# A two-layer graph network on one core: other step orders in both layers, and the last group's row sums as columns

## The chip, the core and the metric

One core of a Trainium2 chip runs the whole program. The metric is the device time of one execution in microseconds; of several runs of a kernel the median is given. One more execution was taken by the hardware profiler; all rows below are from that one.

## The reference

The inputs are x (128 graphs of 128 nodes with 512 features, float32) and adj (128 matrices of 128x128). Two layers follow each other:

```
# layer 0
agg = (adj @ x) / max(rowsum(adj), 1e-6)
x   = layernorm(x + relu(concat(x, agg) @ W.T))
# layer 1
e   = leaky_relu(sj[None, :] + si[:, None] + ab, 0.2)     # scores of x @ Wv + bv with aw
T   = adj * exp(e);  T = T / (rowsum(T) + 1e-12)
H   = x @ Wk[0] + bk[0] + (T @ x) @ Wk[1] + bk[1] + (T @ T @ x) @ Wk[2] + bk[2]
out = layernorm(x + relu(H))
```

Everything is float32.

## The kernel before, in words

**Tiling.** The 128 graphs are taken in 32 groups of four (`G`, `NG`). Group n of 0 to 31 is layer 0, of 32 to 63 layer 1. The 512-feature products use a seven-product (Strassen-like) scheme on two levels: the outer one has the products P12, P56, P74 and `last` (the steps "t") in layer 0, and O1, O2, O5, O6, O7, O4, O3 in layer 1; each of these has seven inner products, its steps 1 to 7. One step is a matmul (or two) and the instruction of VectorE (DVE), ScalarE (ACT) or both that takes its result out of PSUM. One float32 matmul shows in the trace as two passes.

**Banks.** PSUM's eight banks are two lanes of four, `lanes[0]` (bB) and `lanes[1]` (bA). A product calls its lane's banks X, Y, W, Z. In `outer` (line 617) step 1 writes X, and ACT copies X to Y (L628); step 2 writes Z, copied to s5 (L634); step 3 adds to X, and DVE makes W = X + s5 (L637); step 4 finishes Y, which is evicted; step 5 adds to X again, and DVE takes X out (L663 or L676); step 6 finishes W, step 7 X. So step 3 must wait for step 1's copy, step 5 for step 3's add, step 7 for step 5's read. O5 begins with a copy of the bias into X (L626). In `last` (layer 0) X and Z are the two halves of one bank, Y and W of another: t.1 writes X (read by L397), t.2 Z (L400, L401), t.3 X (L404), t.5 X (L409), t.7 X (L416); t.8 to t.11 multiply with the graph's matrix, and `residual` (L380) takes them out.

**Layer 1's second half, `combine` (the steps "c").** For each graph b: `one(b)` multiplies with T into a bank, DVE adds two pieces of the product's result to it and writes v1 (L829, L830), and ACT copies a third piece into the bank (L831); `two(b)` multiplies v1 with T on top of that piece. Group g's steps c run inside group g + 1's list, those of the last group at the end of its own, where they are called x.1 to x.8 (PL).

**The order of the work.** Nothing is left to a scheduler: every engine executes its instructions in program order, and that order is written out. The lists PF, PA (layer 0), PT (last layer-0 group and start of layer 1), PG, PB (layer 1) and PL (last group) give the order of the steps. All other work (transposes `x_turn`, sums `x_inner`, `x_s1` to `x_s4`, degrees, normalisations, loads and stores) is hung between the steps by the PLACES tables: a number is a slot counted from the start of the group's list, two slots to a step; the even slot lies right behind the step's own instructions, the odd one behind the instructions that the step defers (`late`). PA has 32 steps (64 slots), PB 57 (114); a slot beyond that falls into a later group. DMAs are all issued on SyncE (SP) in that same order. PLACES_S (around the change of layers), PLACES_L (last group), PLACES_M and PLACES_T (loads of the second layer's weights) replace or add places.

**The last group's end.** There is no time for a round trip through memory for the scores, so `end_scores` (from L746) makes the diagonal of si (L730), spreads it over all partitions by a matmul with ones, and ACT makes exp of the scores with sources on partitions (L752, L754). `end_rows` multiplies with the adjacency (L760) and spreads the row sums over all partitions, again by a matmul with ones, 256 columns for each half (two graphs). `end_norm` adds epsilon (L768), takes the reciprocal of all 128x256 numbers (L769) and multiplies (L770). Then come x.1 to x.8, the statistics and the stores.

**Start.** Line 151 multiplies the identity into all eight banks once.

Of the kernel before, what the change touches and what calls it, by code (L numbers as in the profile page):

```python
# [16 lines left out]
def kernel(  # L17
# [15 lines left out]
    P = 128  # L33
# [25 lines left out]
    def need(*keys):  # L59
        for k in keys:  # L60
            assert k in done, k
# [89 lines left out]
    for t in bA + bB:  # L151
        nc.tensor.matmul(t, ident, ident[:, None, :].to_broadcast([P, Q, P]), start=True, stop=True)
# [603 lines left out]
    def end_rows(g, h):  # L756
        need(("end_scores", g), ("adj_turn",))
        T = TTs[g][:, 2 * h : 2 * h + 2].rearrange("p b n -> p (b n)")
        pt = lanes[0][1 + h][:, :FH]
        V.tensor_mul(T, T, adjs[2 * NG - 1][:, 2 * h : 2 * h + 2].rearrange("p b n -> p (b n)"))  # L760
        mm(pt, ones[:].to_broadcast([P, P]), T, True)

    def end_norm(g, h):
        need(("end_rows", g, h))
        T = TTs[g][:, 2 * h : 2 * h + 2].rearrange("p b n -> p (b n)")
        pt = lanes[0][1 + h][:, :FH]
        rr = halves()[:, :FH]
        V.tensor_scalar(rr, pt, ROW_EPS, None, ALU.add)  # L768
        V.reciprocal(rr, rr)  # L769
        V.tensor_mul(T, T, rr)  # L770
# [41 lines left out]
    def combine(lane, g):  # L812
        n = NG + g
        X, Y, W, Z = lane
        at_ = {0: X, 1: Z, 2: W, 3: Y}
# [8 lines left out]
        def one(b):  # L824
            need(("end_norm", g, b // 2) if g == NG - 1 else ("t_turn", g))
            need(("O4" if b > 1 else "O3", g, 7), ("sum_c", g, 0), ("sum_c", g, 1))
            mm(at_[b], TTs[g][:, b], row(b, 0, F, 0), True)
            v = v1[b] = v1s[(g * G + b) % 3]
            V.tensor_add(v[:, :258], at_[b][:, :258], row(b, F, 2 * BW, 0))  # L829
            V.tensor_add(v[:, 258:], at_[b][:, 258:], row(b, 0, 254, 1))  # L830
            L_.copy(at_[b], row(b, 254, 766, 1))  # L831

        def two(b):
            mm(at_[b], TTs[g][:, b], v1[b])
            late.append((residual, n, b, at_[b]))
# [15 lines left out]
    def step(lane, name, g, k):  # L851
# [3 lines left out]
    PA = "p74.5 P12.1 P12.2 p74.6 P12.3 p74.7 P12.4 t.1 P12.5 P12.6 t.2 P12.7 P56.1 t.3 P56.2 t.4 t.5 P56.3 t.6 t.7 t.8 t.9 t.10 t.11 P74.1 P74.2 P56.4 P56.5 P56.6 P74.3 P56.7 P74.4".split()  # L855
    PT = "p74.5 p74.6 O1.1 O1.2 O1.3 p74.7 O1.4 t.1 O1.5 O1.6 t.2 O1.7 O2.1 t.3 O2.2 t.4 t.5 O2.3 t.6 t.7 t.8 t.9 t.10 t.11 O2.4 O2.5 O2.6".split()
    PG = ("O5.1 O5.2 O5.3 O5.4 O2.5 O2.6 O6.1 O6.2 O5.5 O5.6 O5.7 O7.1 O6.3 O6.4 O7.2 "
          "O6.5 O2.7 O7.3 O6.6 O7.4 O6.7 O4.1 O4.2 O7.5 O4.3 O7.6 O7.7 O4.4 c.1 O4.5 "
          "O4.6 c.2 c.3 c.4 O4.7 O3.1 O3.2 O3.3 O3.4 c.5 c.6 c.7 c.8 O3.5 O3.6").split()
    PB = ("O1.1 o3.7 O1.2 O1.3 O2.1 O1.4 O1.5 O1.6 O2.2 O1.7 O2.3 O2.4 O5.1 O5.2 O2.5 O5.3 O2.6 O5.4 O2.7 "  # L860
          "O6.1 O5.5 O6.2 O5.6 O6.3 O5.7 O6.4 O7.1 O6.5 O6.6 O7.2 O7.3 O6.7 O4.1 O7.4 O7.5 O4.2 O4.3 O7.6 "
          "O4.4 O4.5 O7.7 c.1 O4.6 O4.7 O3.1 O3.2 c.2 O3.3 c.3 c.4 c.5 c.6 c.7 c.8 O3.4 O3.5 O3.6").split()
    PL = ("O1.1 o3.7 O1.2 O2.1 O1.3 O2.2 O1.4 O1.5 O1.6 O1.7 O2.3 O2.4 O5.1 O2.5 O5.2 O2.6 O2.7 O5.3 O5.4 O6.1 O5.5 O6.2 "
# [44 lines left out]
    def place_op(n, pos, name, m, *a):  # L908
# [3 lines left out]
        else:  # L912
# [3 lines left out]
        ("ln_apply", -2, 3): 4, ("ln_var", -2, 0): -9, ("sum_c22", -2): -40, ("ln_scales", -2): -1, ("ln_mean", -2): -15,  # L916
        ("ln_var", -2, 2): -4, ("load_y", -2, 1): -27, ("ln_apply", -2, 2): 10, ("ln_var", -2, 1): -4,
        ("load_y", -2, 0): -31, ("x_s4", -1): -36, ("ln_var", -2, 3): -12, ("x_s1", -1): -66, ("a_load", -2): -65,
        ("a_turn", -2): -36, ("x_s3", -1): -52, ("y_store", -2, 1): 25, ("ln_apply", -2, 1): 15, ("x_turn", 0, 0, 1): -20,
        ("y_store", -2, 0): 32, ("ln_apply", -2, 0): 15, ("load_left", 0, 0): -49, ("ln_apply", -1, 3): 68, ("x_s2", 0): 28,  # L920
        ("x_turn", 0, 1, 1): -37, ("load_adj", 0): 154, ("ln_var", -1, 0): 58, ("sum_c22", -1): 21, ("ln_scales", -1): 62,
        ("ln_mean", -1): 48, ("x_turn", 0, 0, 0): -28, ("ln_var", -1, 2): 55, ("load_y", -1, 1): 38, ("load_y", -1, 0): 40,
        ("ln_var", -1, 1): 55, ("ln_apply", -1, 2): 70, ("x_s1", 0): 5, ("x_turn", 0, 1, 0): -39, ("a_load", -1): 7,
        ("x_turn", 1, 0, 1): 55, ("x_inner", 0, 0): -12, ("a_norm", -1): -23, ("ln_var", -1, 3): 58, ("degree", -1): -48,
        ("a_turn", -1): 27, ("x_s3", 0): 19, ("y_store", -1, 1): 95, ("ln_apply", -1, 1): 79, ("x_inner", 0, 1): -29,
        ("y_store", -1, 0): 100, ("ln_apply", -1, 0): 82, ("load_left", 1, 0): 9, ("x_s1", 1): 97, ("x_turn", 1, 0, 0): 41,
        ("x_s2", 1): 99, ("x_s4", 0): 80, ("load_left", 1, 1): -24, ("x_inner", 1, 1): 61, ("x_turn", 1, 1, 0): 32,
        ("x_s3", 1): 127, ("x_inner", 1, 0): 64, ("x_turn", 1, 1, 1): 47, ("x_s2", -1): -44,
    }
    PLACES_A = {  # L930
        ("x_s4", 0): 35, ("ln_apply", 0, 3): 131, ("x_s2", 1): 86, ("x_turn", 1, 1, 1): 33, ("ln_var", 0, 0): 124,
        ("sum_c22", 0): 87, ("ln_scales", 0): 126, ("w_slot", 0, 1): 24, ("ln_mean", 0): 113, ("x_turn", 1, 0, 0): 33,
        ("ln_var", 0, 2): 124, ("load_y", 0, 1): 100, ("ln_var", 0, 1): 118, ("load_y", 0, 0): 100, ("ln_apply", 0, 2): 134,
        ("x_s1", 1): 67, ("x_turn", 1, 1, 0): 28, ("a_load", 0): 73, ("x_inner", 1, 0): 51, ("a_norm", 0): 36,
        ("ln_var", 0, 3): 115, ("degree", 0): 17, ("load_left", 2, 1): 38, ("w_slot", 0, 0): 4, ("a_turn", 0): 90,
        ("x_s3", 1): 83, ("y_store", 0, 1): 157, ("ln_apply", 0, 1): 140, ("x_turn", 1, 0, 1): 42, ("x_inner", 1, 1): 36,
        ("load_adj", 1): 37, ("y_store", 0, 0): 161, ("ln_apply", 0, 0): 138, ("load_left", 2, 0): 78,
    }
    PLACES_B = {
        ("t_norm", 0): 154, ("sum_r", 0, 1): 81, ("load_y", 0, 0): 170, ("ln_var", 0, 3): 230, ("x_turn", 1, 0, 1): 19,  # L940
        ("t_back", 0): 165, ("x_s1", 1): 66, ("ln_scales", 0): 239, ("t_sums", 0): 149, ("x_turn", 1, 1, 1): 19,
        ("load_left", 2, 0): 82, ("ln_var", 0, 1): 227, ("y_store", 0, 0): 264, ("t_turn", 0): 187, ("ln_var", 0, 2): 224,
        ("sum_c", 0, 0): 109, ("ln_apply", 0, 2): 273, ("ln_apply", 0, 3): 257, ("x_inner", 1, 1): 53, ("ln_var", 0, 0): 235,
        ("t_exp", 0): 140, ("load_left", 2, 1): 70, ("ln_apply", 0, 1): 257, ("y_store", 0, 1): 278, ("x_s2", 1): 68,
        ("x_turn", 1, 1, 0): -5, ("x_s3", 1): 97, ("ln_apply", 0, 0): 242, ("t_load", 0): 123, ("t_scores", 0): 119,
        ("x_turn", 1, 0, 0): 14, ("sum_r", 0, 0): 86, ("x_s4", 0): 42, ("load_adj", 0): 103, ("load_y", 0, 1): 190,
        ("ln_mean", 0): 223, ("sum_c", 0, 1): 115, ("x_inner", 1, 0): 41,
    }
    PLACES_M = {
        ("ln_mean",): 212, ("ln_apply", 3): 234, ("ln_var", 1): 219, ("ln_apply", 0): 250, ("y_store", 0): 251,  # L950
        ("ln_apply", 2): 231, ("ln_var", 2): 225, ("ln_apply", 1): 235, ("ln_var", 3): 225, ("ln_scales",): 230,
        ("y_store", 1): 244, ("ln_var", 0): 227,
    }
    PLACES_L = {
        ("end_store", 2): 158, ("sum_c", 1): 72, ("sum_r", 0): 71, ("end_store", 0): 158, ("t_scores",): 105,
        ("end_var", 1): 134, ("sum_r", 1): 71, ("load_adj",): 96, ("load_y", 0): 47, ("end_apply", 1): 160,
        ("load_y", 1): 106, ("end_mean", 1): 128, ("end_rows", 0): 111, ("end_mean", 0): 127, ("end_rstd", 2): 132,
        ("end_store", 1): 160, ("end_apply", 2): 137, ("end_stats", 2): 129, ("end_store", 3): 162, ("end_scales",): 140,
        ("sum_c", 0): 76, ("end_rstd", 3): 149, ("end_apply", 0): 144, ("end_scores",): 106, ("end_rows", 1): 111,
        ("end_norm", 0): 111, ("end_stats", 3): 138, ("end_norm", 1): 111, ("end_apply", 3): 158, ("adj_turn",): 96,  # L960
        ("end_var", 0): 131,
    }
    OPS = {f.__name__: f for f in (load_left, load_y, load_adj, x_turn, x_inner, x_s1, x_s2, x_s3, x_s4, sum_c22, degree, a_norm, a_load, a_turn, w_slot, ln_mean, ln_var, ln_scales, ln_apply, y_store, sum_r, sum_c, t_scores, t_load,
           t_exp, t_sums, t_norm, t_back, t_turn, end_scores, end_rows, end_norm)}
    ENDS = {f.__name__: f for f in (adj_turn, end_mean, end_var, end_scales, end_stats, end_rstd, end_apply, end_store)}
    LAST = {"ln_mean", "ln_var", "ln_scales", "ln_apply", "y_store"}
    OWN = {"sum_r", "sum_c", "t_scores", "t_load", "t_exp", "t_sums", "t_norm", "t_back", "t_turn", "end_scores", "end_rows", "end_norm"}
# [112 lines left out]
```

## Time and profile before

| what | value |
|---|---|
| median of 3 runs | 2085.56 us (2084.93 to 2086.3) |
| profiled execution: time | 2083.08 us |
| profiled execution: span from first to last instruction | 2081.3 us |
| mean granted TensorE clock | 0.998 |
| PE, DVE, POOL, ACT busy | 99%, 73%, 66%, 56% |
| one group of layer 0, from 137.37 us | 24.74 us |
| one group of layer 1, from 887.61 us | 38.91 us |
| DMA | 287.13 MB, mean 138 GB/s |

A timeline row gives the start (us), the time it covers, engine, line, operation, what is written and read (buffer numbers left out), the shape and the count; a bracket at its end is the idle time of that engine before it and the instruction that ended it. PE is the matmul, PEld the load of its weights. A row of the waits is: engine and line that waited, the one that it waited for, us in total, number of times, longest.

### The profile page before, as it was taken

What the parts mean: (1) busy time and instruction counts of PE and PEld (TensorE: products, weight loads), DVE (VectorE), ACT (ScalarE), POOL (GpSimd) and SP (SyncE); (2) the same over time, 40 slices, a digit from 0 to 9 for tenths busy, and PEclk for the clock granted to TensorE, in tenths of its full rate; (3) what the DMA queues carried; (4) which work ended last, traced back from release to release, by engine and by line L of the source; (5) the groups of instructions that cost most, each with busy time, mean ns of one, the idle gap of its engine ahead of it and who ended that gap; (6) DMA issues with size and microseconds to landing.
All of it is one profiled execution on the core that took longest, in us unless ns stands there. A gap on an engine that the chain in (4) does not pass through costs nothing.

```text
span 2081.3 us, 25875 instructions
## 1 busy us (share of the span) xinstructions
PE 2062.5 (99%) x7096; PEld 1329.9 (64%) x7096; DVE 1525.8 (73%) x3414; ACT 1155.7 (56%) x2875; POOL 1377.7 (66%) x1263
## 2 busy tenths in 40 slices
PE   9999999999999999999999999999999999999997
PEld 6778888888878886555555555555555555555553
DVE  6777777777777777676776776776776776776766
ACT  2656666666666666355455455455455465465464
POOL 5877888887676776656656656656556556556552
PEclk9999999999999999999999999999999999999999
DMA  9776666666667776435434535535535435435423
GB/s 206 174 190 194 180 182 179 160 187 192 163 160 190 190 183 218 107 87 122 116 87 115 124 87 127 112 87 128 111 87 130 109 87 132 107 87 132 107 67 117
DMA packets 431070, 287.13 MB, mean 138 GB/s; under 512 B 155593, under 2 KB 353865, under 8 KB 430924
## 3 DMA queue, kind: packets, MB, share of 16 engines
q1 hardware_dynamic: 429996, 284.15, 54.6%
q10 hardware_dynamic: 800, 1.31, 0.3%
q8 instruction: 56, 0.92, 0.2%
q14 instruction: 90, 0.74, 0.1%
q0 software_dynamic: 128, 0.01, 0.0%
HBM read 191.60 MB, written 93.79 MB: 137 GB/s over the span
## 4 chain that ended last, share of the span: by engine, by line
PE 97%; DVE 1%; DMA 1%; ACT 0%; issue 0%; POOL 0%; SPq 0%; ACTq 0%; DVEq 0%
PE bA L155 51%; PE bB L155 46%; DMA yd<-y 0%; DMA xb<-in_x_dram 0%; DMA y<-in_x_dram 0%; PE bA L181 0%; DVE s L769 0%; DVE y L380 0%; POOL r L709 0%; ACT y L517 0%; DVE big L995 0%; DVE xl L259 0%; DVE xu L259 0%; DVE big L1003 0%; SPq L83 0%
## 5 line engine op out<-in xcount | busy, mean ns | idle before, releaser
L155 PE MATMUL bB<-big,xu 128*128 128x385 f32 (+1 forms) x1806 | 569.5, 435 | 1.0 <-DVE c L676 0.7
L155 PEld LDWEIGHTS bB<-big,xu 128*128 128x128 f32 x1806 | 339.4, 190 | 166.6 <-issue 30.1
L155 PE MATMUL bA<-big,xl 128*128 128x256 f32 (+1 forms) x1358 | 395.9, 416 | 0.3 <-DVE bA L475 0.3
L155 PE MATMUL bB<-big,xs 128*128 128x256 f32 (+1 forms) x1316 | 388.8, 416 | 0.0
L155 PEld LDWEIGHTS bA<-big,xl 128*128 128x128 f32 x1358 | 256.8, 189 | 100.1 <-issue 15.5
L155 PEld LDWEIGHTS bB<-big,xs 128*128 128x128 f32 x1316 | 249.5, 190 | 84.2 <-issue 1.7
L155 PE MATMUL bA<-big,xu 128*128 128x256 f32 (+1 forms) x896 | 290.0, 435 | 0.2
L155 PE MATMUL bA<-c,TT 128*128 128x512 f32 x512 | 245.9, 592 | 3.0 <-DVE c L669 1.9
L504 ACT ACTIVATE junk<-y,mv 128x512 bf16<-128x512 f32 x252 | 181.3, 719 | 72.7 <-POOL mv L499 68.5
L155 PEld LDWEIGHTS bA<-big,xu 128*128 128x128 f32 x896 | 165.4, 189 | 82.2 <-DVE bA L637 9.7
L517 ACT ACTIVATE y<-y,mv,rstd 128x512 f32<-128x512 f32 x252 | 201.5, 812 | 1.4 <-POOL mv L512 1.4
L380 DVE SCALAR_TENSOR_TENSOR y<-bA,y 128x512 f32<-128x512 f32 x256 | 170.4, 683 | 19.6 <-PE bA L155 13.4
L155 PE MATMUL bA<-big,xs 128*128 128x385 f32 x448 | 178.3, 492 | 0.0
L709 POOL TENSOR_TENSOR r<-r,s 128x770 f32<-128x770 f32 x64 | 115.1, 1820 | 86.4 <-DVE c L669 86.4
L155 PE MATMUL bB<-big,xl 128*128 128x385 f32 (+1 forms) x462 | 167.2, 480 | 0.5 <-ACT bA L456 0.4
L155 PEld LDWEIGHTS bA<-c,TT 128*128 128x128 f32 x512 | 96.8, 189 | 93.0 <-issue 48.1
L790 POOL TENSOR_TENSOR T<-ag,T 128x512 f32<-128x512 f32 x31 | 39.5, 1275 | 175.9 <-ACT T L785 175.9
L499 POOL TENSOR_SCALAR mv<-mv 128x4 f32<-128x4 f32 x63 | 14.5, 230 | 212.3 <-DVE y L380 212.3
L270 POOL TENSOR_TENSOR xs<-xl 128x896 f32<-128x896 f32 x63 | 131.4, 2086 | 23.9 <-PE bB L155 23.9
L282 POOL TENSOR_TENSOR xu<-xu,xs 128x896 f32<-128x896 f32 x63 | 131.8, 2091 | 8.8 <-PE bB L155 8.8
L831 ACT COPY bA<-r 128x512 f32<-128x512 f32 x64 | 37.7, 590 | 176.4 <-DVE big L830 170.7
L637 DVE TENSOR_TENSOR bB<-bB,s 128x385 f32<-128x385 f32 x128 | 72.5, 567 | 85.1 <-PE bB L155 75.4
(190 smaller groups left out, 3636.7 us busy)
## 6 DMA issues: line engine op xcount, KB each, us to landing
xb<-in_x_dram SPq DMA_DIRECT2D x256, 128.0 KB, 3.8
y<-in_x_dram SPq DMA_DIRECT2D x64, 512.0 KB, 4.3
yd<-y SPq DMA_DIRECT2D x64, 512.0 KB, 3.0
xb<-yd SPq DMA_DIRECT2D x256, 128.0 KB, 5.8
y<-yd SPq DMA_DIRECT2D x64, 512.0 KB, 5.9
out_dram<-y SPq DMA_DIRECT2D x62, 512.0 KB, 2.8
ag<-in_adj_dram SPq DMA_DIRECT2D x63, 256.0 KB, 5.9
sb<-sd SPq DMA_DIRECT2D x252, 64.0 KB, 3.2
```

Of the source, the lines that this page charges most:

```text
L155: nc.tensor.matmul(dst, lhsT, rhs, start=start, stop=True, skip_group_check=True)
L270: S_.tensor_add(xs[n][:, 0], xl[n][:, 0], xl[n][:, 1])
L282: S_.tensor_sub(xu[n][:, 1], xu[n][:, 1], xs[n][:, 1])
L380: V.scalar_tensor_tensor(y, t, 0.0, y, ALU.max, ALU.add, accum_out=mvs[n][:, b, 0:1])
L499: S_.tensor_scalar(mvs[n][:, :, 0], mvs[n][:, :, 0], -1.0 / F, None, ALU.mult)
L504: L_.activation(junk, ys[n, b // 2][:, b % 2], AF.Square, bias=mvs[n][:, b, 0:1], accum_out=mvs[n][:, b, 1:2])
L517: L_.activation(y, y, AF.Identity, bias=mvs[n][:, b, 0:1], scale=rstds[n][:, b : b + 1])
L637: V.tensor_add(W, X, s5)
L709: S_.tensor_add(r, r, s)
L790: S_.tensor_mul(T, adjs[NG + g], T)
L831: L_.copy(at_[b], row(b, 254, 766, 1))
```

## The change

- PF and START are as they were. PA, PT, PG, PB and PL contain the same steps in another order, and the numbers of the PLACES tables are set anew.
- The last group's row sums: `end_rows` now multiplies with the one-column `ones` as moving operand, so the sums of one graph are one column on the partitions of the rows, four columns in one bank. `end_recip` (new) adds epsilon and takes reciprocals of 128x2 numbers and writes two diagonals; `end_norm` spreads those by a matmul with ones (256 columns, same bank) and multiplies from PSUM.
- `end_base` (new): for graphs 0, 1 and 2 of the last group the third piece is put into banks of the other lane by a matmul with the identity ahead of time; `two(b)` adds to it there. The ACT copy L831 remains for graph 3 in that group and everywhere in the others.
- The matmul of the identity at the start covers seven banks, not eight.

```diff
-    for t in bA + bB:
+    for t in bA + bB[:3]:
...
     def end_rows(g, h):
-        need(("end_scores", g), ("adj_turn",))
+        need(("end_scores", g), ("adj_turn",), *[("end_rows", g, 0)] * h)
+        T, pt = TTs[g], lanes[0][0]
+        t2 = T[:, 2 * h : 2 * h + 2].rearrange("p b n -> p (b n)")
+        V.tensor_mul(t2, t2, adjs[2 * NG - 1][:, 2 * h : 2 * h + 2].rearrange("p b n -> p (b n)"))
+        for b in (2 * h, 2 * h + 1):
+            mm(pt[:, b : b + 1], T[:, b], ones, b == 0)
+
+    def end_recip(g, h):
+        need(("end_rows", g, 1))
+        t = lanes[0][0][:, 2 * h : 2 * h + 2]
+        rr = small.tile([P, 2], FP, name="rr2")
+        V.tensor_scalar(rr, t, ROW_EPS, None, ALU.add)
+        V.reciprocal(rr, rr)
+        if h == 0:
+            ends["dr"] = p1.tile([P, G, N], FP, name="dr", tag="sb")
+        for b in (0, 1):
+            V.tensor_scalar(ends["dr"][:, 2 * h + b], ident, rr[:, b : b + 1], None, ALU.mult)
+
+    def end_norm(g, h):
+        need(("end_recip", g, 1), *[("end_norm", g, 0)] * h)
         T = TTs[g][:, 2 * h : 2 * h + 2].rearrange("p b n -> p (b n)")
...
+        pt = lanes[0][0][:, h * FH : (h + 1) * FH]
+        mm(pt, ones[:].to_broadcast([P, P]), ends["dr"][:, 2 * h : 2 * h + 2].rearrange("p b n -> p (b n)"), h == 0)
+        V.tensor_mul(T, T, pt)
+
+    def end_base(g, b):
+        need(("sum_c" if b > 1 else "O3", g, 0 if b > 1 else 7))
+        t = (rs[NG + g], last22[g])[b // 2][:, b % 2].rearrange("p n m -> p (n m)")
+        mm(lanes[0][1 + b], ident, t[:, 254:766], True)
...
-        at_ = {0: X, 1: Z, 2: W, 3: Y}
+        at_ = to = {0: X, 1: Z, 2: W, 3: Y}
+        if g == NG - 1:
+            to = {0: lanes[0][1], 1: lanes[0][2], 2: lanes[0][3], 3: X}
...
-            L_.copy(at_[b], row(b, 254, 766, 1))
+            if g < NG - 1 or b == 3:
+                L_.copy(to[b], row(b, 254, 766, 1))
 
         def two(b):
-            mm(at_[b], TTs[g][:, b], v1[b])
-            late.append((residual, n, b, at_[b]))
+            need(*[("end_base", g, b)] if g == NG - 1 and b < 3 else [])
+            mm(to[b], TTs[g][:, b], v1[b])
+            late.append((residual, n, b, to[b]))
...
-    PA = "p74.5 P12.1 P12.2 p74.6 P12.3 p74.7 P12.4 t.1 P12.5 P12.6 t.2 P12.7 P56.1 t.3 P56.2 t.4 t.5 P56.3 t.6 t.7 t.8 t.9 t.10 t.11 P74.1 P74.2 P56.4 P56.5 P56.6 P74.3 P56.7 P74.4".split()
+    PA = "p74.5 P12.1 p74.6 P12.2 P12.3 p74.7 t.1 P12.4 P12.5 t.2 P12.6 P12.7 P56.1 t.3 P56.2 t.4 t.5 P56.3 t.6 t.7 t.8 t.9 t.10 t.11 P74.1 P56.4 P74.2 P56.5 P56.6 P74.3 P56.7 P74.4".split()
-    PT = "p74.5 p74.6 O1.1 O1.2 O1.3 p74.7 O1.4 t.1 O1.5 O1.6 t.2 O1.7 O2.1 t.3 O2.2 t.4 t.5 O2.3 t.6 t.7 t.8 t.9 t.10 t.11 O2.4 O2.5 O2.6".split()
+    PT = "p74.5 p74.6 O1.1 O1.2 O1.3 p74.7 t.1 O1.4 O1.5 O1.6 t.2 O1.7 O2.1 t.3 O2.2 t.4 t.5 t.6 O2.3 t.7 t.8 O2.4 O2.5 t.9 O2.6 t.10 t.11".split()
...
-    PB = ("O1.1 o3.7 O1.2 O1.3 O2.1 O1.4 O1.5 O1.6 O2.2 O1.7 O2.3 O2.4 O5.1 O5.2 O2.5 O5.3 O2.6 O5.4 O2.7 "
-          "O6.1 O5.5 O6.2 O5.6 O6.3 O5.7 O6.4 O7.1 O6.5 O6.6 O7.2 O7.3 O6.7 O4.1 O7.4 O7.5 O4.2 O4.3 O7.6 "
-          "O4.4 O4.5 O7.7 c.1 O4.6 O4.7 O3.1 O3.2 c.2 O3.3 c.3 c.4 c.5 c.6 c.7 c.8 O3.4 O3.5 O3.6").split()
+    PB = ("O1.1 o3.7 O1.2 O1.3 O2.1 O1.4 O1.5 O2.2 O1.6 O1.7 O2.3 O2.4 O5.1 O5.2 O2.5 O5.3 O2.6 O5.4 O5.5 "
+          "O2.7 O6.1 O5.6 O6.2 O6.3 O5.7 O6.4 O7.1 O6.5 O6.6 O7.2 O6.7 O7.3 O4.1 O7.4 O7.5 O4.2 O4.3 O7.6 "
+          "O4.4 O4.5 O7.7 O4.6 c.1 O4.7 O3.1 c.2 c.3 O3.2 c.4 c.5 c.6 O3.3 c.7 c.8 O3.4 O3.5 O3.6").split()
```

Of the places, those that the prediction speaks of (slot before, slot after). PLACES_A: degree 17, 19; x_turn (1,1,0) 28, 26; x_turn (1,1,1) 33, 30; x_turn (1,0,0) 33, 32; a_turn 90, 95 (26, 31 of the next group); a_load 73, 81; load_left (2,0) 78, 93; sum_c22 87, 80. PLACES_B: x_turn (1,0,1) 19, 29; x_turn (1,1,0) -5, -5; t_scores 119, 121; t_load 123, 126; t_sums 149, 151; t_norm 154, 154; t_back 165, 167; t_turn 187, 189; y_store (0,1) 278, 284; load_left (2,0) 82, 88. PLACES_L: end_scores 106, 108; end_base (2), (0), (1) new at 110, 111, 112; end_rows 111, 111; end_recip new at 111, 112; end_norm (0) 111, 113, (1) 111, 115. In PG, O4.5 to O4.7 read `O4.5 O4.6 ... O4.7` before (the steps c between them are empty in that group) and `O4.5 O7.7 O4.6 ... O4.7` after.

## Prediction

> **What bounds the kernel now.** I read the page first, then the waits of PE's weight loads, then the timeline of one steady group of each layer and of the end.
>
> ```profile
> span 2081.3 us, 25875 instructions
> PE 2062.5 (99%) x7096; PEld 1329.9 (64%) x7096; DVE 1525.8 (73%) x3414; ACT 1155.7 (56%) x2875; POOL 1377.7 (66%) x1263
> ```
>
> TensorE is the bound. A pass over 256, 385 or 512 columns takes 216, 324 or 430 ns from start to start (eight of 256 from 143.84 to 145.57; six of 385 from 890.96 to 892.90; two of 512 from 920.22 to 921.07), and a float32 product is two passes. Counting all passes at that price gives 2038 us, so 43 us of the span is not passes: 9 lie behind the last product, some 19 in waits at the start, at the change of layers and in the last group, and 15 in tiny waits that come back in each group of a layer (0.16 x 31 and 0.33 x 30, below). Most of those never show as idle PE. They show on the weight load: when a semaphore comes so late that the weights are not loaded ahead, a pass is some 100 ns late.
>
> ```profile
> PEld bA L155 <- ACT bA L831: 23.8, 37, 1.6
> PEld bB L155 <- DVE r L676: 14.1, 30, 0.8
> ...
> PEld bA L155 <- DVE s L401: 8.8, 31, 0.3
> ```
>
> The middle number is the count: 30 or 31 is once a group. Layer 0, one group:
>
> ```profile
> 146.38 0.16 DVE L599 TENSOR_REDUCE deg<-deg 128x4 f32<-128x8 f32 x1 [0.62 <-ACT junk L597]
> 146.86 1.03 PE L155 MATMUL bB<-big,xs 128*128 128x256 f32 x4
> 147.32 0.41 DVE L401 TENSOR_TENSOR s<-bA,s 128x256 f32<-128x256 f32 x1
> 147.78 0.30 PEld L155 LDWEIGHTS bA<-big,xu 128*128 128x128 f32 x2 [0.29 <-DVE s L401]
> 147.78 0.70 PE L155 MATMUL bA<-big,xu 128*128 128x256 f32 x2
> 148.32 1.03 PE L155 MATMUL bB<-big,xs 128*128 128x256 f32 x4
> ```
>
> Step P56.1 starts at 146.86 and needs 4 x 0.216, so t.3 could start at 147.72; it starts at 147.78, and its two passes last 0.54, not 0.43. Sum 0.16 us a group. The cause is the first row: `degree` stands in DVE's order ahead of t.2's two adds (L400, L401), and DVE sits 0.62 us waiting for ACT's sums.
>
> Layer 1, one group:
>
> ```profile
> 887.06 0.70 DVE L259 STREAM_TRANSPOSE xl<-xb 128x512 f32<-128x512 f32 x1
> 887.69 0.52 DVE L676 TENSOR_TENSOR r<-bB,r 128x385 f32<-128x385 f32 x1
> 888.26 0.30 PEld L155 LDWEIGHTS bB<-big,xu 128*128 128x128 f32 x2 [0.46 <-DVE r L676]
> ...
> 894.92 0.50 ACT L626 COPY bA<-beta 128x385 f32<-128x385 f32 x1
> 895.57 1.53 PE L155 MATMUL bA<-big,xs 128*128 128x385 f32 x4
> ...
> 897.79 0.56 DVE L676 TENSOR_TENSOR c<-bB,c 128x385 f32<-128x385 f32 x1
> 898.43 0.57 DVE L637 TENSOR_TENSOR bA<-bA,s 128x385 f32<-128x385 f32 x1
> ```
>
> Three places: o3.7 waits for L676 behind a transpose (0.10 us), O5.1 for the bias copy L626 behind the copy out of O1.7 (0.16), c.8 for c.5's copy L831 (six passes from 883.03 to 885.67 take 2.64 against 2.58: 0.07). The end:
>
> ```profile
> 2060.43 1.75 DVE L769 RECIPROCAL s<-s 128x256 f32<-128x256 f32 x1
> 2062.70 1.13 PE L155 MATMUL bA<-c,TT 128*128 128x512 f32 x2 [1.04 <-DVE TT L770]
> 2063.01 1.75 DVE L769 RECIPROCAL s<-s 128x256 f32<-128x256 f32 x1
> 2065.74 1.98 PE L155 MATMUL bA<-c,TT 128*128 128x512 f32 x4 [1.92 <-DVE c L669]
> 2069.65 2.98 PE L155 MATMUL bA<-big,TT 128*128 128x512 f32 x6
> ```
>
> **Layer 0 (PA, PLACES_A): -4.9 us.** `degree` goes from slot 17 to 19, behind t.2's adds, and t.2 to t.3 now has P12.6, P12.7, P56.1 between. From the group's start: t.2 ends at 7.77, L401 at 8.9, t.3 is due at 10.36, so its 0.16 us goes: x 31 = 4.9. What is late next: the transposes. x_turn twice and a_turn now all stand between t.3's add L404 (at 11.0) and t.5's L409: 11.0 + 0.34 + 3 x 0.63 = 13.23, end 13.65; t.7, which overwrites what L409 reads, is due at 13.82. A release must come 0.10 ahead to cost nothing (o3.7: released just when PE is free, 0.10 late), and 0.12 is left. I take nothing; the bound is 0.10 x 31 = 3.1. ACT's degree now delays P12.6's copies to 9.4; their reader P56.2 is due at 10.8. a_load moves behind sum_c22 and ahead of load_left on SP; in the trace SP runs its loads some 9 us ahead of the transposes, so nothing. The other steps and POOL's sums keep their distances.
>
> **Layer 1 (PB, PG, PLACES_B): -0.8 us.** c.8: O3.3 is put between c.6 and c.7, +0.65 us of cover against a lack of 0.07: gone, 30 x 0.07 = -2.2. O5.1: O1.7, O2.3, O2.4, O5.1 keep their order, ACT still has a 0.7 us normalisation and three copies ahead of L626 (893.1 + 0.36 + 0.71 + 0.37 + 0.37 = 894.9, as now): stays. o3.7: the transpose at slot -5 and the tail c.8 O3.4 O3.5 O3.6 O1.1 stay: 0.10 stays. New: x_turn (1,0,1) goes from slot 19 to 29, onto DVE between L676 and L637 above. L637 then starts at 897.79 + 0.47 + 0.63 = 898.89, ends at 899.42, seen by PE at 899.47; O5.5, now only two steps behind O5.3, is due at 899.53. 0.06 ahead where 0.10 is needed (a release 0.13 ahead, L637 for O1.5 at 891.47, costs nothing now): 0.05 x 30 = +1.4. If that transpose is the 0.70 of its longest rows, it is 0.12 (+3.6); if the row's gaps shrink, nothing. Behind L637 wait L669 of O2.6 and, through it, the row sums of `t_sums`, with 0.4 us to spare at O6.5. The turn of the scores moves behind O1.3's add (DVE waited 0.97 for ACT there), t_load 1.5 steps later; ACT reads it 0.7 later too.
>
> **Change of layers (PT, PLACES_S, PLACES_T): -0.6 us.** The PE rows from 806 to 849 hold 3.1 us over their passes. O4.5 to O4.7 gets O7.7 between: -0.27. The largest, 0.96 at O2.7, is L676 queued behind residuals that wait for y's DMA; L676 now stands ahead of three of them, but O5.2 and O5.3 need those residuals themselves, so I give nearly all of it back there, and count half of the 0.53 behind it (O6.2, O5.6). Bounds: -2.5 (all single-step waits covered) and +1.5 (each of the four residuals a full step late). One filler matmul on bB[3] less at the start: 0.43 x 2 passes, but A.2 waits for DVE's w_inner until 12.44 anyway: 0.
>
> **Last group (PL): -0.3 us, end: -1.8 us.** O1.3's add no longer waits behind the turned scores: 0.27 at 2021.9. The end: O4.4 runs ahead of end_scores, in its wait (0.94 + 0.1), so nothing moves on the chain scores, exp, which still starts at 2057.05 and gives half 1 at 2059.1. The two 1.75 us reciprocals go; in their place per half an add and a reciprocal on 128x2 (0.19 each by the 128x4 row L601) and two diagonals (0.21 each, L730: 4 in 0.86). PE adds three 512-column matmuls with the identity (0.86 each = 2.6, two of them in waits that exist), eight passes of one column, two of 256 twice. For one column the nearest row is the eight 2-column passes at 55.14 in 1.05: 0.13 each, 1.0 in all. The Trainium skill (TensorE: Matmul & The Clock Gate, "Wait — 56ns, not 53.3ns?") states a floor of about 25 ns between matmuls, which would make it 0.2; I take the row, since every pass loads 128 columns of new weights. Then PE runs from O4.5 at 2056.79: 0.65 + 2 x 0.86 + 1.0 (to 2060.15), O4.6 0.65, base 0.86 (2061.66), first broadcast (its diagonal is ready at 2061.1, held to 2060.7 by ACT's square in the same buffer), done 2062.35; O4.7 to 2063.0. The Trainium skill (PSUM — Partial Sum Buffer, "PSUM bank collisions raise a hardware error") says that two engines must be kept apart on a bank even in disjoint columns; the L401 row obeys it (t.3 writes the other half of that bank). All of rows, sums and broadcasts now share one bank, so the second broadcast waits for the first product: 2063.02 to 2063.56. Without the rule it would be 0.4 less. Then x.1 to x.8 have no copies in their way, 8 x 0.86: the seventh ends at 2069.6 and its residual starts at 2069.8; now it is 2071.57: -1.8. Behind it the chain to the last store is the same, so the end moves by that. ACT's three copies of 0.59 go. New on ACT: the previous group's last square shares its buffer with the diagonals and waits for the second broadcast (2063.56); behind it stand three normalisations and x.5's copy, done by 2068.5, which x.8 needs at 2069.6.
>
> **Sum.** 4.9 + 0.8 + 0.6 + 0.3 + 1.8 = 8.4 us from the profiled execution's 2083.08 (span 2081.3): 2074.7. The median lies 2.48 above that execution: 2085.56 - 8.4 = 2077.2.
>
> **Rivals.**
> *The transposes eat it (0.15).* t.7 and O5.5 each a full 0.1 late: +3.1 and +1.6 more, and the change of layers at +1.5 (2.1 more): 2077.2 + 6.8 = 2084.0, no change. For: margins of 0.02 and -0.04 us. Against: both are worked from median rows, and a little idle elsewhere gives DVE time.
> *More is gained (0.12).* O5.1 and o3.7 go too: 30 x 0.26 = 7.8 more: 2069.4. For: every place of the layer is set anew. Against: the ACT and DVE orders ahead of both are the same.
> *Slower: SP's queue (0.06).* t_back now stands ahead of y_store, load_y and load_left, and t_norm comes later on ACT: store at 903.5, in at 911.2, while t_turn is at 913.4 and DVE's adds for O4.4 to O4.7 stand behind it. It decides if that load lands 2.2 us later than worked out; at 0.5 us a group it is +15: 2092.
> *Forecast as worked out: 0.67*, 2074.5 to 2080.
>
> The range reaches to part of the first two rivals: 2071.5 to 2083. About 0.2% (4.2 us) is what a measurement can tell from no change; faster than 2081.4: 0.67 + 0.12 + a little of the first rival = 0.81; within: 0.12; slower: 0.07.
>
> **What shows it.** Right: L401 gone from the weight loads' waits, the group of layer 0 at 24.59 us (24.75 now); L831 once or twice, not 37 times; layer 1's group at 38.88 (38.91); the once-a-group wait for L637 moved from O1.5 to O5.5; no 1.75 us reciprocal, last residual near 2071 of a span 8 us shorter. Wrong: a once-a-group wait for L409 (t.7), waits at c.1 for t_turn, or the end no shorter because the broadcasts queue in their one bank.

## The result, and the profile after

The median went from 2085.56 us (five runs, 2084.46 to 2086.85) to 2074.95 us (five runs, 2074.79 to 2076.03): ratio 0.995, 95% interval 0.9935 to 0.9964. The two profiled executions are 2083.08 and 2074.86 us (spans 2081.3 and 2073.1). So the profiles differ by 8.2 us and the medians by 10.6; the last experiments explain that gap. The bound is still TensorE, by the first rows of the page after:

```profile
span 2073.1 us, 25953 instructions
PE 2059.1 (99%) x7108; PEld 1334.4 (64%) x7108; DVE 1528.9 (74%) x3418; ACT 1158.6 (56%) x2872; POOL 1377.5 (66%) x1263
```

Where it came from is read by the start of one and the same pass in both traces (us from the span's start):

| pass | before | after | difference | gained since the row above |
|---|---|---|---|---|
| P56.1 of layer 0's last group of the PA list | 790.26 | 786.83 | -3.43 | 3.4, layer 0 |
| second O5.1 of layer 1 | 856.74 | 851.37 | -5.36 | 1.9, change of layers |
| 31st O5.1 | 1985.48 | 1979.16 | -6.32 | 1.0, layer 1 |
| O5.1 of the last group | 2024.63 | 2018.13 | -6.50 | 0.2 |
| last residual (L380) | 2073.13 | 2064.74 | -8.39 | 1.9, last group and end |
| span | 2081.30 | 2073.07 | -8.23 | -0.2, last stores |

Over 30 groups each, the median group of layer 0 went from 24.746 to 24.611 us, that of layer 1 from 38.912 to 38.892.

**Layer 0.** The timeline of one group after, with the rows that answer to those of before:

```profile
144.21 0.30 PEld L155 LDWEIGHTS bA<-big,xu 128*128 128x128 f32 x2 [0.15 <-DVE bA L397]
144.30 0.62 PE L155 MATMUL bA<-big,xu 128*128 128x256 f32 x2
...
145.44 0.41 DVE L401 TENSOR_TENSOR s<-bA,s 128x256 f32<-128x256 f32 x1
146.26 0.84 PEld L155 LDWEIGHTS bB<-big,xs 128*128 128x128 f32 x4
146.40 0.16 DVE L599 TENSOR_REDUCE deg<-deg 128x4 f32<-128x8 f32 x1 [0.55 <-ACT junk L597]
146.48 1.03 PE L155 MATMUL bB<-big,xs 128*128 128x256 f32 x4
...
147.13 0.41 PEld L155 LDWEIGHTS bA<-big,xu 128*128 128x128 f32 x2
147.34 0.59 PE L155 MATMUL bA<-big,xu 128*128 128x256 f32 x2
```

L401 now ends ahead of the wait for ACT's sums (L599), and t.3 starts at 147.34, 0.86 behind P56.1 (146.48): 4 x 0.216, nothing over. Its weights start to load 0.21 ahead of it. But t.2's (144.30) start only 0.09 ahead, for they wait for L397: 0.02 us a group are lost anew.

**Layer 1.** The same view, one group:

```profile
882.31 0.52 DVE L676 TENSOR_TENSOR r<-bB,r 128x385 f32<-128x385 f32 x1
882.88 0.30 PEld L155 LDWEIGHTS bB<-big,xu 128*128 128x128 f32 x2 [0.46 <-DVE r L676]
882.88 0.92 PE L155 MATMUL bB<-big,xu 128*128 128x385 f32 x2
...
890.19 1.53 PE L155 MATMUL bA<-big,xs 128*128 128x385 f32 x4
...
893.51 0.53 DVE L637 TENSOR_TENSOR bA<-bA,s 128x385 f32<-128x385 f32 x1
894.10 0.30 PEld L155 LDWEIGHTS bA<-big,xs 128*128 128x128 f32 x2 [0.40 <-DVE bA L637]
```

In the first three rows o3.7's weights start to load together with the pass that needs them (both at 882.88), and its two passes take 0.92 for 0.81. In the last two rows O5.5 waits for L637 as forecast. The excess of a step is the time from its start to the next one's beyond the 216, 324 or 430 ns of its passes. Averaged over 30 groups it is: o3.7 0.102, O5.1 0.154 (0.082 at the end of O2.4, 0.072 within), O5.5 0.054; c.8's 0.074 is gone.

**The waits** of the weight loads in the page's order, after:

```profile
PEld bA L155 <- ACT bA L849: 16.9, 63, 1.6
PEld bB L155 <- DVE r L676: 13.7, 30, 0.5
PEld bA L155 <- DVE bA L637: 12.5, 32, 0.4
```

L401 is gone from these, with 0.2 us in a single wait. The copy that was L831 (now L849) still stands there, 63 times of 0.27, though its loss is gone: a wait of 0.24 of a weight load is what every load between two 512-column passes shows (0.43 from start to start, 0.19 for the load). This list says what to look at, not what is lost.

**The end**, timeline after:

```profile
2049.26 1.12 PE L155 MATMUL bB<-dg,ones 128*128 128x512 f32 x2
2052.59 1.05 PE L155 MATMUL bB<-ones,TT 128*128 128x1 f32 x8
2053.88 0.17 DVE L769 RECIPROCAL rr<-rr 128x2 f32<-128x2 f32 x1
2054.15 0.48 DVE L773 TENSOR_SCALAR dr<-ident,rr 128x128 f32<-128x128 f32 x2
...
2055.22 0.70 PE L155 MATMUL bB<-dr,ones 128*128 128x256 f32 x2
2055.95 0.42 DVE L780 TENSOR_TENSOR TT<-TT,bB 128x256 f32<-128x256 f32 x1
2056.43 0.30 PEld L155 LDWEIGHTS bB<-dr,ones 128*128 128x128 f32 x2 [0.48 <-DVE TT L780]
2056.97 2.74 PE L155 MATMUL bA<-c,TT 128*128 128x512 f32 x6
```

The eight one-column passes take 0.91 us to O4.6's start; the weight load of the second broadcast waits 0.48 for the product that reads the first from the same bank; and from 2056.97 TensorE has no gap up to its last product. The two reciprocals of 1.75 us are gone.

### The profile page after: what moved, and what is told of

It is laid out like the page before. It is cut to its first block, busy times and chain, and to the rows that moved or that the text cites. A ratio compares the mean times of both kernels' runs of the same rounds, so it can differ in the third digit from the quotient of the medians.

```text
span 2073.1 us, 25953 instructions
## 1 busy us (share of the span) xinstructions
PE 2059.1 (99%) x7108; PEld 1334.4 (64%) x7108; DVE 1528.9 (74%) x3418; ACT 1158.6 (56%) x2872; POOL 1377.5 (66%) x1263
## 4 chain that ended last, share of the span: by engine, by line
PE 58%; DVE 0%; POOL 0%; ACT 0%; issue 0%; ACTq 0%
PE bA L155 31%; PE bB L155 27%; POOL r L709 0%; DVE r L669 0%; ACT y L562 0%; POOL rs L539 0%; DVE dg L730 0%; DVE y L380 0%; ACTq L1096 0%; DVE st L546 0%; ACT bA L849 0%; POOL rs L555 0%; DVE r L673 0%; ACT s L634 0%; DVE big L847 0%
## 5 line engine op out<-in xcount | busy, mean ns | idle before, releaser
L155 PE MATMUL bA<-big,xl 128*128 128x256 f32 (+1 forms) x1358 | 406.0, 416 | 0.3 <-DVE bA L475 0.3
L155 PE MATMUL bA<-c,TT 128*128 128x512 f32 x512 | 240.9, 592 | 0.0
L380 DVE SCALAR_TENSOR_TENSOR y<-bA,y 128x512 f32<-128x512 f32 x253 | 168.1, 682 | 30.1 <-PE bA L155 24.4
L155 PE MATMUL bB<-big,xl 128*128 128x385 f32 (+1 forms) x462 | 172.0, 480 | 0.4 <-ACT bA L456 0.4
L499 POOL TENSOR_SCALAR mv<-mv 128x4 f32<-128x4 f32 x63 | 14.5, 230 | 234.8 <-DVE y L380 234.8
L637 DVE TENSOR_TENSOR bB<-bB,s 128x385 f32<-128x385 f32 x128 | 72.6, 567 | 130.1 <-ACT s L634 52.0
L849 ACT COPY bA<-r 128x512 f32<-128x512 f32 x62 | 36.6, 590 | 190.3 <-DVE big L847 155.1
L669 DVE TENSOR_TENSOR r<-bB,r 128x385 f32<-128x385 f32 x192 | 106.5, 555 | 43.6 <-PE bB L155 40.0
```

Source lines behind the costliest of these rows:

```text
L155: nc.tensor.matmul(dst, lhsT, rhs, start=start, stop=True, skip_group_check=True)
L380: V.scalar_tensor_tensor(y, t, 0.0, y, ALU.max, ALU.add, accum_out=mvs[n][:, b, 0:1])
L499: S_.tensor_scalar(mvs[n][:, :, 0], mvs[n][:, :, 0], -1.0 / F, None, ALU.mult)
L637: V.tensor_add(W, X, s5)
L669: V.tensor_add(part(dst, b, BW), t, part(src, b, BW))
L849: L_.copy(to[b], row(b, 254, 766, 1))
```

## The experiments

Ratios are to the kernel before, run beside each (its medians there: 2084.6 to 2084.9 us). Groups and excesses are worked out from the passes' starts. The kernel after was not run again beside these; where a run is compared with it, that is with its median of 2074.95, and the groups in the run's own trace stand beside it.

**One part alone, three times.** Layer 0: before with PA and PLACES_A of after. Layer 1: before with PB and PLACES_B. The end: after with all other lists and places put back.

```diff
-    PA = "p74.5 P12.1 P12.2 p74.6 P12.3 p74.7 P12.4 t.1 P12.5 P12.6 t.2 P12.7 P56.1 t.3 ...
+    PA = "p74.5 P12.1 p74.6 P12.2 P12.3 p74.7 t.1 P12.4 P12.5 t.2 P12.6 P12.7 P56.1 t.3 ...
...
-        ("degree", 0): 17
+        ("degree", 0): 19
```

> The kernel before with only layer 0's step order and places (PA, PLACES_A) taken from the changed one. If each wait has its own cause: the group of layer 0 goes from 24.75 to 24.61 us, L401 leaves the weight loads' waits, and the whole is 3.5 to 4 us faster (span 2077.5); layer 1's group stays at 38.91 and the end as it was. If the parts only work together (the places at the change of layers belong to the new order): new waits at the change of layers eat at least 2 us of it.

Measured: 2080.9 us, 0.9982 (0.9975 to 0.9989). The group is 24.609; the last P56.1 comes 3.47 us earlier, all that after gains there. But the second O5.1 comes only 2.34 earlier: with the old places the change of layers takes back 1.1. DVE's waits for the old y say why; for this kernel, from 795 to 835 us, in us and times:

```profile
  DMA y<-in_x_dram: 5.6, 3
```

Before, it is `2.9, 2`; after shows no such wait.

```diff
-    PB = ("O1.1 o3.7 O1.2 O1.3 O2.1 O1.4 O1.5 O1.6 O2.2 O1.7 ...
+    PB = ("O1.1 o3.7 O1.2 O1.3 O2.1 O1.4 O1.5 O2.2 O1.6 O1.7 ...
...
-        ("x_turn", 1, 0, 1): 19
+        ("x_turn", 1, 0, 1): 29
```

> The kernel before with only layer 1's step order and places (PB, PLACES_B) taken from the changed one. Own causes: L831's once-a-group wait goes, a wait of 0.05 us at O5.5 comes, O5.1 and o3.7 stay; the group goes from 38.91 to 38.89 us, so the whole is only 0.5 to 1 us faster (span 2080.5), plus what the change of layers has of it. Rival, layer 1's order carries most of the 8.2 us: span below 2077.

Measured: 2084.21 us, 0.9997 (0.9989 to 1.0005), no difference by this measurement. The group is 38.891: c.8 gone, O5.5's 0.054 new, o3.7 and O5.1 as before. The span is 2081.7, not 2080.5; its profile holds one window of halved clock at the end, which costs 1.16 us (last section).

The end alone keeps `end_recip`, `end_norm`, `end_base`, PL and PLACES_L of after, and has of before:

```diff
-    PA, PT, PG, PB; PLACES_S, PLACES_A, PLACES_B, PLACES_T   # of after
+    PA, PT, PG, PB; PLACES_S, PLACES_A, PLACES_B, PLACES_T   # of before
```

> The changed kernel with all orders and places of layer 0, of the change of layers and of layer 1's groups put back; the last group's list, its places, the row sums as columns and the bases put in by PE stay, and seven filler matmuls. Own causes: the last group ends some 2.3 us earlier than before counted from its own start, span 2079. Rival, the gain at the end is the new order of the last group's steps and not the columns: cannot be told by this run, its groups show the same either way; rival, the end gains nothing alone: 2081.

Measured: 2080.84 us, 0.9982 (0.9974 to 0.999). From the last group's O5.1 to the last pass it gains 2.15 us, to the end of the span 1.9, with groups as before. The median gains 4.1, 1.6 more than the span's 2.5. The columns, the bases by TensorE and the new list PL come together here; no run tells them apart.

**The place of degree**, alone in each direction:

```diff
-        ("degree", 0): 17     # e2_degree: before, degree put behind t.2's adds in the old order
+        ("degree", 0): 21
...
-        ("degree", 0): 19     # e3_degree_back: after, with the old place
+        ("degree", 0): 17
```

> The kernel before with one number changed: degree from slot 17 to slot 21, behind t.2's two adds, the step order as before. If the degree's place ahead of t.2's adds is the cause of t.3's wait: the group of layer 0 goes to 24.6 us and the span falls by 4 to 4.7 us (2077). If the cause is the distance from t.2 to t.3 (two steps before, three after): 24.75 stays, span 2081.

Measured: 2088.04 us, 1.0016 (1.0009 to 1.0022): slower, which neither of the two expectations had. t.3's excess goes, and a larger one appears a step later, at P56.2 and t.4 (0.166 and 0.104; group 24.859). The wait of the weight loads, this kernel:

```profile
PEld bA L155 <- DVE bA L404: 12.7, 31, 0.5
```

DVE's wait for ACT's sums now stands ahead of t.3's add L404.

> The changed kernel with degree put back from slot 19 to slot 17, ahead of t.2's two adds; the new step order stays. The run with degree alone moved showed the wait shift from t.3 to t.4 and grow. If the new distance from t.2 to t.3 (three steps, not two) and the place of degree are both needed: t.3 waits again, some 0.1 to 0.25 us a group, the group of layer 0 goes from 24.61 back to 24.7 to 24.85, the whole 3 to 7 us slower than the changed kernel. If the step order alone did it: 24.61 stays, no difference.

Measured: 2081.87 us, 0.9987 (0.9981 to 0.9994), group 24.88. Either half of the edit alone makes the group longer than the 24.746 of before; only together do they give 24.61. With both, the wait stands behind t.2's adds, and three steps (P12.6, P12.7, P56.1) lie between t.2 and t.3.

**What after still loses in layer 1.** Two transposes moved two slots back, each alone, then both; then the normalisation that stands ahead of O5.1's bias copy on ACT.

```diff
-        ("x_turn", 1, 0, 1): 29     # e6_turn, e9_both, e10_all
+        ("x_turn", 1, 0, 1): 31
-        ("x_turn", 1, 1, 0): -5     # e8_turn2, e9_both, e10_all
+        ("x_turn", 1, 1, 0): -3
-        ("ln_apply", 0, 0): 242     # e7_norm: 256; e10_all: 280, with
+        ("ln_apply", 0, 0): 280     #   ("y_store", 0, 0): 263 -> 282
```

> The changed kernel with one transpose of layer 1, x_turn (1,0,1), moved from slot 29 to 31, so that it follows O5.3's add L637 on VectorE. If that transpose makes O5.5's wait of 0.05 us: it goes, the group of layer 1 falls from 38.89 to 38.84, the whole 1.5 us. If the wait comes from the shorter distance O5.3 to O5.5: it stays.

Measured: 2073.12 us, 0.9945 (0.9932 to 0.9957). O5.5's excess is gone and the group is 38.838; 1.8 us below after.

> The changed kernel with x_turn (1,1,0) of layer 1 moved from slot -5 to slot -3, behind the read L676 that o3.7 waits for. If the transpose ahead of L676 makes o3.7's late weight load: its 0.10 us goes, the group falls to 38.79, the whole 3.1 us faster; rival: the transpose then delays O3.6's eviction and the wait moves to a step of the next group, no gain.

Measured: 2071.42 us, 0.9936 (0.9924 to 0.9949), 3.5 below after; group 38.780. In its timeline L676 now runs ahead of the transpose, and o3.7 is on time:

```profile
882.03 0.56 DVE L676 TENSOR_TENSOR r<-bB,r 128x385 f32<-128x385 f32 x1
...
882.51 0.70 DVE L259 STREAM_TRANSPOSE xl<-xb 128x512 f32<-128x512 f32 x1
882.81 0.51 PEld L155 LDWEIGHTS bB<-big,xu 128*128 128x128 f32 x2
883.13 0.81 PE L155 MATMUL bB<-big,xu 128*128 128x385 f32 x2
```

The weights load 0.32 ahead, and the two passes take 0.81.

> The changed kernel with one normalisation of layer 1, ln_apply (0,0), moved from slot 14 to slot 28 of its group, out of ScalarE's queue ahead of the bias copy L626. If O5.1's wait of 0.16 us is made by ScalarE's queue: it falls to 0 to 0.05, the group of layer 1 goes to 38.73 to 38.78, the whole 3.5 to 4.7 us faster. If it is the product's own chain (O1.7's end, its copy, the bias copy): no change.

Measured: 2077.82 us, 0.9967 (0.9954 to 0.9979), 2.9 slower than after. O5.1's 0.154 is gone, so ACT's queue was its cause; but at its new place the normalisation joins two others and the five instructions of `t_exp`, and O6.1's copy L628 is late: O6.2 loses 0.137 and O6.3 0.100, a group is 38.977. Its new row among the waits of the weight loads:

```profile
PEld bB L155 <- ACT bB L628: 18.5, 32, 0.6
```

> The kernel after with both transposes moved: x_turn (1,0,1) two slots later and x_turn (1,1,0) two slots later. Theory (each late release costs its own 0.05 to 0.12 us once a group, independent of the others): the two savings measured singly, 1.8 and 3.5 us, add up: 2069.6 us, and the layer-1 group is 38.72 us (38.89 now, 38.84 and 38.78 with one of them). Rival (PE that runs ahead at one place only arrives earlier at the next late release, at O5.1, which is set by ACT's queue): at most the larger saving, 2071.4 us, with O5.1 above its 0.154 us.

Measured: 2070.0 us, 0.9931 (0.9918 to 0.9945); group 38.727. The two savings add up: in the group 0.054 + 0.112 against 0.165, in the whole to within 0.4 us.

> As before it, and the normalisation ln_apply (0,0) moved 38 slots later, into ACT's idle stretch at O7.1 of the next group, with the first y_store behind it. Theory (O5.1 is late only because that normalisation stands ahead of the bias copy on ACT, and a place with idle ACT costs nothing): O5.1's 0.154 us goes too, 30 x 0.154 = 4.6 us: 2065.0 us, layer-1 group 38.57 us. Rival (ACT's queue only passes the delay on, as the shorter move of the same instruction did, or the later store delays the loads behind it on SP): 2069 to 2072 us, with a new once-a-group wait for an ACT copy or for a residual.

Measured: 2064.78 us, 0.9906 (0.9893 to 0.992), 10.2 below after; group 38.567, with no step's mean excess above 0.02 left. At O5.1 the bias copy now has only ACT's copies ahead of it, and the four passes take 1.46 for 1.53:

```profile
888.65 0.48 ACT L660 COPY r<-bA 128x385 f32<-128x385 f32 x1 [0.17 <-PE bA L155]
889.03 0.49 ACT L626 COPY bA<-beta 128x385 f32<-128x385 f32 x1
...
889.75 1.46 PE L155 MATMUL bA<-big,xs 128*128 128x385 f32 x4
```

**The gap between profile and median.** The kernel before once more:

> The kernel before once more, for a second profile. If the profiled execution of before was a short one (2083.08 against medians of 2084.7 to 2085.6), this one is 2084.5 to 2086, with the extra time in single pauses that the first does not have. If instead profiled executions of this kernel are always about 2 us shorter than its median, it is 2082.8 to 2083.4.

Measured: 2085.28 us, span 2083.5. Up to the last group's O4.1 it even lies 0.31 us ahead of the first profile; the last pass lies 2.00 behind. The windows view (window, its length, busy us of PE, PEld, DVE, ACT and POOL, granted clock, DMA share, GB/s), first of the first profile, then of this one:

```profile
2060.90:2064.31 3.41, 1.88 (x5) 0.43 (x3) 3.34 (x4) 0.59 (x2) 1.43 (x3) 1.00 0.00 0
2064.31:2067.72 3.41, 1.98 (x4) 0.68 (x4) 3.23 (x8) 0.54 (x2) 0.00 (x0) 1.00 0.00 0
```

```profile
2060.97:2064.38 3.41, 1.50 (x4) 0.30 (x2) 3.34 (x4) 0.21 (x2) 1.43 (x3) 1.00 0.00 0
2064.38:2067.79 3.41, 2.36 (x3) 1.17 (x4) 2.34 (x7) 0.90 (x2) 0.00 (x0) 0.50 0.01 2
2067.79:2071.21 3.42, 3.42 (x5) 1.35 (x4) 1.52 (x5) 2.14 (x4) 0.00 (x0) 0.50 0.00 0
```

While TensorE waits for the two long reciprocals it is busy for 1.88 us of a window in the one and for 1.50 in the other; in the second its clock is then halved for 6.83 us, right over the products x.2 to x.5. Is it the waiting that does it? Fill the waits with matmuls into an unused bank:

```diff
             need(("O4" if b > 1 else "O3", g, 7), ("sum_c", g, 0), ("sum_c", g, 1))
+            for _ in range((1, 2, 0, 0)[b] if g == NG - 1 else 0):
+                mm(lanes[0][3], ident, ident[:, None, :].to_broadcast([P, Q, P]), True)
             mm(at_[b], TTs[g][:, b], row(b, 0, F, 0), True)
```

> The kernel before with three matmuls of the identity into an unused bank, in the waits of TensorE at its end: one ahead of x.1 (0.86 us in a wait of 1.04) and two ahead of x.2 (1.73 us in a wait of 1.92). Nothing else differs. Theory (the executions of before differ because the granted clock is halved, for 0, 3.4 or 6.8 us, in some of them while TensorE waits for the two long reciprocals; busy TensorE keeps the clock): the clock stays 1.00 to the last product, the median is that of the first profile, 2083.1 us (2082.8 to 2083.6), and the runs lie within 1 us of each other, against 2082.6 to 2085.8 for before. Rival (the spread of before comes from elsewhere, or the fillers only delay x.1 and x.2): median 2084.7 us or more, with the same spread of 3 us.

Measured: 2083.28 us (13 runs, 2082.66 to 2083.87) beside 2084.66 of before (17 runs: five from 2082.95 to 2083.10, twelve from 2084.22 to 2085.77). The ratio, 0.9994 (0.9986 to 1.0003), doesn't tell them apart by itself; the spread of 1.2 us for 2.8 (1 was expected), the absence of anything above 2083.9, and the clock do. The last pass starts as far behind O4.1 as in the first profile (21.05 us), the clock is 1.00 until 3.8 us behind the last product, and the window of the second wait now reads:

```profile
2063.24:2066.65 3.41, 3.20 (x7) 1.28 (x8) 3.34 (x6) 0.00 (x0) 0.31 (x2) 1.00 0.00 0
```

The run with the new end alone says the same: its 15 runs lie within 0.8 us (2080.58 to 2081.38), the 17 of layer 0 alone, with the old end, within 2.8 (2079.54 to 2082.37).

## Why the prediction came out, point by point

**The total** of 2077.2 was 2.2 us too high, because the distance of 2.48 us between profile and median was carried over as if it were a constant. It was no constant: it was the halved clock at the end. After's median lies 0.09 us above its own profile. Against the profile alone, 2083.08 - 8.4 = 2074.7 was forecast and 2074.86 measured, but that closeness is partly luck: layer 0 gave 1.5 us less and the change of layers 1.3 more.

| term | forecast | profile | what was off |
|---|---|---|---|
| layer 0 | -4.9 | -3.4 | size |
| change of layers | -0.6 | -1.9 | a wait said to come back did not |
| layer 1 | -0.8 | -1.0 | a single pause of before beside it |
| last group | -0.3 | -0.2 | size near, wrong wait |
| end | -1.8 | -1.7 | nothing |

**Layer 0, -4.9:** the mechanism was right (the wait left t.3; both the order and the place are needed, by the two runs on `degree`). The term "0.16 x 31" was mis-sized: the loss before was 0.153 a group, the new one at t.2 is 0.022, and the median group falls by 0.135; 29 groups gain it, 3.9 in all. Two single pauses, which only the new order has, take the rest: 0.10 at 150.8 us, where t.7 waits for L409 once, and 0.37 at 685.6 us. There DVE starts an add (L320) 0.35 us later than in the group before, just behind the end of a POOL instruction, and t.2's add L397 comes late with it; why only there is open. The forecast had not asked about t.2's add, only about the transposes. These were its worry, with 0.12 us of margin where 0.10 is needed: t.7 shows no excess but in that one group, so the rival "the transposes eat it" fell, in its layer-0 half.

**Layer 1, -0.8:** each of its three steps held: c.8's 0.07 gone, o3.7's 0.10 and O5.1's 0.15 stayed, O5.5 lost 0.054 where 0.05 was forecast. That is 0.020 a group, 0.6 in all; 0.36 more is one pause that before has at 1043.6 us, in both of its profiles, and after has not. In the trace DVE's L669 sits idle there for 0.37 us until POOL's L499 ends, and o3.7 comes late by as much; why only in that group is open. The sign "L831 once or twice" did not come (63 times); it asked the waits for what only the starts of the passes show. The rival "more is gained" was wrong for this kernel, and right as to what can be had: the runs that moved the two transposes and the normalisation got it.

**Change of layers, -0.6:** the failed step is "I give nearly all of it back there": the forecast took it that the residuals' wait for y's DMA would stay and only move from O2.7 to O5.2 and O5.3. It left. Before and after, DVE's first residual that waited and the last of the four:

```profile
821.28 0.69 DVE L380 SCALAR_TENSOR_TENSOR y<-bA,y 128x512 f32<-128x512 f32 x1 [2.37 <-DMA y<-in_x_dram]
823.75 0.69 DVE L380 SCALAR_TENSOR_TENSOR y<-bA,y 128x512 f32<-128x512 f32 x1 [0.55 <-DMA y<-in_x_dram]
```

```profile
818.32 0.67 DVE L380 SCALAR_TENSOR_TENSOR y<-bA,y 128x512 f32<-128x512 f32 x1
820.02 0.65 DVE L380 SCALAR_TENSOR_TENSOR y<-bA,y 128x512 f32<-128x512 f32 x1
```

The change of PLACES_S also moved the load of y: SP issues the two at 811.1 and 814.3 us after, 814.3 and 819.9 before, and the slowest lands in 4.5 us instead of 6.9. Counted from O5.1, the second load is issued 1.7 us earlier. The forecast had moved DVE's instructions, not SP's. With the old places and the faster layer 0 the wait doubles (5.6 us in the run of layer 0 alone), so the new lists and places are worth more than the 1.9 shows: 3.1 us from P56.1 to the second O5.1, against that run. One new wait, which no term held, counts against them: 0.65 us at O1.7 of layer 1's second group, where L663 stands behind a transpose on DVE. No run changes the lists and places of this part alone, so its account rests on the traces.

**Last group, -0.3:** the forecast named the 0.27 at 2021.9 and O1.3's add. In before's trace the weight load there waits for L663, which reads O1.5's result before O1.7 overwrites it, with only O1.6 between. PL keeps O1.5 to O1.7 together, so this wait stays (0.27 at 2015.6 after). What left is 0.23 at O5.1.

**End, -1.8:** the last O4.1 comes 6.57 us earlier than before and the last residual 8.39, so 1.82, as worked out. Of the single terms, the row's 0.13 for a one-column pass came to 0.114, and the Trainium skill's 25 ns (TensorE: Matmul & The Clock Gate, "Wait — 56ns, not 53.3ns?") is far from passes that load new weights each time; its rule that two engines keep off one bank even in disjoint columns (PSUM — Partial Sum Buffer, "PSUM bank collisions raise a hardware error") is what the program keeps, with 0.48 us of wait at the second broadcast. In the last stores 0.16 is lost. What the forecast did not see is the other half of this part: it keeps TensorE busy, so the clock is not halved before the last product in any profile with the new end. (The sign "last residual near 2071" counted this part alone; with the other terms it is 2064.7, and 2064.74 was measured.) **Slower: SP's queue** did not happen: no wait at the steps c for `t_turn`.

## What to carry to other kernels

A wait of 0.1 us that recurs in each group can be removed by moving one instruction in an engine's order, but ask first what will stand behind it at the new place and who waits for that: moving one instruction some slots later was worth -3.5, -1.8, +2.9 or +3.1 us here. Read such losses from the starts of the passes, not from the sum of the waits. And where single runs of a kernel differ by more than its profile explains, take a second profile and compare the granted clock window by window before anything is forecast from the distance between profile and median.

## What the runs showed of the hardware that was not expected

- **The clock is halved for whole windows, and a window less than half busy can be enough.** Within each trace all changes of the clock lie whole multiples of 3.413 us apart, from its rise at the start to its falls at the end. Three falls lie ahead of the last product, behind windows in which TensorE was busy for 1.12, 1.49 and 1.50 us of 3.41 (the runs of layer 1 and of `degree` at 21, the second profile of before); behind windows with 1.88, 1.93 and 1.98 it stayed. It came back after a window with 3.01 us busy or more, not after one with 2.36: so after one window (3.41 us, costing 1.16 us in the runs of layer 1 and of `degree` at 21) or two (6.83 us, 2.31 us in the second profile of before). Where the limit lies is open, and the busy time alone does not give it: in windows that begin with the last products it fell behind 1.49, 1.55 and 1.60 us (before, layer 0, layer 1) but stayed behind 1.64 and 1.42 (both transposes moved; the normalisation moved too). The run of layer 0, then the one with the normalisation moved too:

```profile
2068.39:2071.80 3.41, 1.55 (x4) 0.30 (x2) 2.80 (x9) 2.64 (x6) 1.17 (x4) 1.00 0.39 154
2071.80:2075.21 3.41, 0.00 (x0) 0.00 (x0) 1.56 (x4) 1.52 (x2) 1.73 (x4) 0.50 0.78 297
```

```profile
2052.88:2056.29 3.41, 1.42 (x4) 0.35 (x2) 2.80 (x9) 2.04 (x4) 1.12 (x4) 1.00 0.33 126
2056.29:2059.70 3.41, 0.00 (x0) 0.00 (x0) 1.68 (x4) 1.52 (x2) 1.79 (x5) 1.00 0.84 313
```

The Trainium skill (TensorE: Matmul & The Clock Gate, "What's actually happening") states a window of 3413 ns that runs free of the program, which these traces agree with: counted from the last O4.1, the window that holds the wait ahead of x.1 begins at 9.90 us in the first profile of before and at 10.28 in the second, so that it holds 0.38 us less of work. Its advice against idle gaps beyond about 3 us (the same page, "Why this matters for your kernels") does not cover this case: the longest single gap between products was 1.92 us. (Busy times rest on modelled ends of the passes.)

- **A weight load that comes late costs up to 0.105 us between two passes though TensorE never idles** (o3.7, t.3, the second pass of each broadcast): started 0.09 ahead of the pass (t.2) it costs 0.02, 0.21 ahead (t.3 after) nothing.
